# Second cross attention of a Perceiver block on one core: attention weights transposed in 32 by 32 blocks instead of by matrix multiplication

## The chip, the cores and the metric

The kernel runs on one core of a Trainium2 chip. The core has five engines that run side by side: TensorE (PE in the profile, its weight loads PEld) multiplies matrices into PSUM, VectorE (DVE), ScalarE (ACT) and GpSimd (POOL) work on elements, and SyncE (SP) issues most DMAs. Each engine executes its own instructions in program order. The metric is the device time of one execution in microseconds (us).

## What is computed

The reference is a chain of layers on `x`, 32 batches of 64 tokens with 256 features, and a context of 256 rows for each batch, all in float32. The layers are a cross attention with 16 heads of 64 (the first one), a linear attention, a gated feed forward, a second cross attention with 16 heads of 16, an sLSTM recurrence along the 64 tokens, and a mixture of 8 experts with an entmax router. The change lies in the second cross attention:

```python
Q = (query @ Wq.T + bq) ; K = (key @ Wk.T + bk) ; V = (value @ Wv.T + bv)     # 16 heads of 16
energy = einsum('bhqd,bhkd->bhqk', Q, K) / sqrt(16)
energy = where(mask == 0, -1e20, energy)
attention = softmax(energy, axis=-1)
out = einsum('bhqk,bhkd->bhqd', attention, V) ... @ Wo.T + bo
```

Since each row of `attention` sums to 1, the bias `bv` adds the same vector `bv @ Wo.T` to every token.

## The kernel before

The 2048 tokens are 16 tiles of 128 rows, two batches to a tile. First the kernel does the first cross attention for all tiles. Then come 8 groups of two tiles; for each group it does the linear attention, the feed forward, the second cross attention and the sLSTM with the router. At the end the experts run, part A over the first 12 tiles and part B over the rest.

**The planner.** The code doesn't issue instructions in the order in which it is written. `Plan` (lines 210 to 381) collects all operations with a rank (`pl.rank`), an estimated length (`PlanEngine.length`, lines 452 to 472) and their dependencies. `run` (line 299) then simulates the engines and issues at each step the operation that can start earliest, by rank among equals. Operations whose rank lies more than `ahead` over the lowest waiting one are held back; `pl.run(12.0)` on line 1863 sets that. Every instruction is issued on line 375, so all of them have the line L375 in the profile, and they are told apart by tile and shape. `either` (line 288), and `copy` by it, leave the choice between ScalarE and VectorE to the planner. `together` makes one planned piece of several matmuls, and pieces with the same `pl.lane` stay in order on TensorE. Tiles in SBUF have fixed places in one large arena, named in the lists from line 588 on: each entry has a tag, a size and one or more places, and the number of places is the number of buffers. A new tile waits until the last reader of its place is done. PSUM has eight banks, taken in any order.

**The first cross attention** already transposes its weights in blocks (`l0_scores`, line 869): VectorE transposes 32 by 32 blocks of `pr` into `bT`, and 16 moves of 32 partitions each put the blocks in their places in `pT`. Of these four go to GpSimd, four to ScalarE or VectorE, and eight are DMAs from SP. `bT` has one buffer and `pT` two.

**The second cross attention** works in units of one tile `t` and one half `c` of the heads, 32 units in all. `scores` (line 1274) multiplies queries and keys into four PSUM banks; each bank holds two heads for both batches. For each of the eight pieces of 128x256 VectorE adds the mask and takes the maximum in one operation (`tensor_tensor_reduce`, line 1298, shown as CUSTOM_DVE_ANT_0), and ScalarE takes the exponential into `pr` (`xpr`, two buffers of 2048) with the row sums. `weighted` (line 1313) then transposes the 16 blocks of 128x128 on TensorE (line 1324, PSUM tile `xpTp`), four to a bank, copies each bank to SBUF by `pl.copy` (line 1325, tile `xpT`), and multiplies by the values into `po` (line 1340, `xpo`). VectorE multiplies by the transposed reciprocal sums and adds the two heads of a pair and the values' bias in one instruction (line 1349). `projected` multiplies by the output matrix. `slstm_router` (line 1365) has its clamp, sums and product on VectorE (lines 1405 to 1415).

**Constants.** `vb` (line 1035) holds the values' bias as a column, made by a product with the identity and a sum.

Of the kernel before, what the change touches and what calls it, by code (L numbers as in the profile page):

```python
# [8 lines left out]
F32 = mybir.dt.float32  # L9
I32 = mybir.dt.int32  # L10
AF = mybir.ActivationFunctionType
ALU = mybir.AluOpType
# [197 lines left out]
class Plan:  # L210
# [12 lines left out]
    def __init__(self, tc):  # L223
        self.tc, self.ops, self.slots, self.news = tc, [], {}, []
        self.rank, self.group, self.lane, self.last = 0.0, None, None, {}
        for engine, attr in self.ENGINES.items():
            setattr(self, attr, PlanEngine(self, engine))
# [71 lines left out]
    def run(self, ahead):  # L299
# [7 lines left out]
        while todo:  # L307
# [3 lines left out]
            for op in sorted(ready, key=lambda op: op.rank):  # L311
                if short is not None and op.rank > short.rank and "PE" in op.ways and op.news:
                    continue
                if op.rank > rest[-1].rank + ahead:
                    continue
                at = 0.0
                if op.news and not self.has_room(op):
                    if "PE" in op.ways and (short is None or op.rank < short.rank) and self.has_room(op, True):
                        short = op
                    continue  # L320
                for engine, (length, _) in op.ways.items():
                    at = free[engine]
                    for other in op.before:
                        at = max(at, other.end if other.on == engine and other.end == other.done else other.done + self.HOP)
                    for t_ in op.uses:
                        at = max(at, t_.free_at)
                    key = at, op.rank
                    if best is None or key < best[0]:
                        best = key, op, engine
# [109 lines left out]
class PlanEngine:  # L439
# [34 lines left out]
    def length(engine, name, args, kw):  # L474
# [18 lines left out]
        if engine == "POOL":  # L493
            return 0.7 if n < 64 else 0.3 + 2.0e-3 * n
        return 0.18 if name == "transpose" else max(0.36, 1.67e-3 * n)
# [3 lines left out]
def kernel(ctx: ExitStack, tc: tile.TileContext, d: dict, out: bass.AP):  # L499
# [130 lines left out]
    with ExitStack() as sa:  # L630
# [31 lines left out]
        for tag, size, *at in (  # L662
# [8 lines left out]
            ("xcT", 1024, 22016, 23040), ("xkT", 1024, 24064, 25088), ("xv", 1024, 30208, 31232),  # L671
            ("xpr", 2048, 26112, 28160), ("xpT", 512, 35328, 35840, 36352, 36864), ("xne", 256, 37376, 37632, 37888),
            ("xra", 256, 38144, 38400), ("xrT", 256, 38656, 38912), ("mi", 256, 39168), ("xom", 256, 39424, 39680),
# [36 lines left out]
        def bank(shape, name):  # L710
            return banks.tile(shape, F32, tag="a", name=name)
# [143 lines left out]
        def l0_keys(b, lt, cx):  # L855
# [11 lines left out]
            return cT  # L867

        def l0_scores(b, cT, qk):

# [5 lines left out]
            pl.lane = "s"  # L876
            B_ = 32
            bT = ar.tile([P, 5, 4, 4, B_], F32, tag="bT", name=f"bT{b}")
# [32 lines left out]
            for n in range(4):  # L911
                for a in range(4):
# [4 lines left out]
                    )  # L917
                    if n == 0:
                        pl.gpsimd.tensor_copy(o, i_)
                    elif n < 2:  # L920
                        pl.copy(o, i_)
                    else:
                        pl.sync.dma_start(out=o, in_=i_)
            return pT
# [117 lines left out]
        )  # L1042
        pl.vector.tensor_reduce(vb, vd, AX.X, ALU.add)

        pl.vector.tensor_scalar(s_wp, s_wp, 0.5, None, ALU.mult)
# [228 lines left out]
        def scores(t, c, q, kT):  # L1274

            pl.lane = "sc"
            nm = f"{t}_{c}"
            pl.rank = R0 + 2 * t + c - 0.5
            sm = sp.tile([P, 2, 4], F32, tag="xsm", name=f"xsm{nm}")
            pr = ar.tile([P, 2, 4, S2], F32, tag="xpr", name=f"xpr{nm}")  # L1280
            scs = [bank([P, 2, S2], f"xsc{nm}_{j}") for j in range(4)]
            with pl.together(1.45):
                for b2 in range(2):
                    for j in range(4):
# [8 lines left out]
                        )  # L1293
            for j in range(4):
                for b2 in range(2):
                    ne = ar.tile([P, S2], F32, tag="xne", name=f"xne{nm}_{j}_{b2}")
                    nmax = sp.tile([P, 1], F32, tag="xnm", name=f"xnm{nm}_{j}_{b2}")
                    pl.vector.tensor_tensor_reduce(ne, scs[j][:, b2, :], mb, 1.0, 3.0e38, ALU.add, ALU.min, nmax)
                    pl.scalar.activation(
                        pr[:, b2, j, :], ne, AF.Exp, bias=nmax, scale=-1.0, accum_out=sm[:, b2, j : j + 1]  # L1300
                    )
# [8 lines left out]
            )  # L1310
            return ra, pr

        def weighted(t, c, ra, pr, v, oT):
            pl.lane = "w"
            nm = f"{t}_{c}"
            pl.rank = R0 + 2 * t + c
            pTs = {}
            for b2 in range(2):
                for kc in range(2):
                    pT = ar.tile([P, 4, P], F32, tag="xpT", name=f"xpT{nm}_{b2}_{kc}")  # L1320
                    pT_ps = bank([P, 4, P], f"xpTp{nm}_{b2}_{kc}")
                    with pl.together(T4):
                        for j in range(4):
                            tr(pT_ps[:, j, :], pr[:, b2, j, kc * P : (kc + 1) * P], ident)
                    pl.copy(pT, pT_ps)
                    pTs[b2, kc] = pT

# [37 lines left out]
        def slstm_router(g):  # L1365
# [49 lines left out]
            pl.vector.tensor_tensor(iz[:, :, 1:], tmp2, z, ALU.mult)  # L1415
            pl.vector.tensor_tensor_scan(flat(c_), flat(fs), flat(iz), 0.0, ALU.mult, ALU.add)
# [32 lines left out]
        for g in range(NG):  # L1449
# [3 lines left out]
            for t in range(TG * g, TG * g + TG):  # L1453
                kT, v = keys_values(t)
                oT = ar.tile([P, 2, 2, S], F32, tag="xoT", name=f"xoT{t}")
                for c in range(2):
                    ra, pr = scores(t, c, q, kT)
                    weighted(t, c, ra, pr, v, oT)
                projected(t, oT)
# [402 lines left out]
        v.tensor_copy(nbi, nbf)  # L1862
        pl.run(12.0)
        n_more = nc.values_load(  # L1864
# [69 lines left out]
```

## Time and profile before

| | us |
|---|---|
| median of three timed runs | 1628.32 (1628.05 to 1630.23) |
| time of the profiled execution | 1633.02 |
| its span, first to last instruction | 1631.3 |
| TensorE busy in it | 1579.4 |
| VectorE busy | 1088.2 |
| ScalarE busy | 693.8 |
| GpSimd busy | 422.1 |

The profiled execution has a time of its own, 4.7 us over the median of the timed runs; durations from its trace are set against this time. In the lines of the profile, `out<-in` names the written and read tiles; all arena tiles have the one name `arena`, and PSUM tiles have the names of the code (`xpTp`, `xsc`, `pu`). Behind them stand the shape, the count, the busy time in us and the mean duration of one instruction in ns. Behind the last bar stands the time that the engine sat idle just before these instructions, and what ended it. Busy time counts overlapping instructions once, so for pipelined matmuls it is less than count times mean.

### The profile page before, as it was taken

How to read it: one execution, taken by the hardware profiler on the slowest of the kernel's cores; microseconds unless marked ns; L12 is line 12 of the kernel's file. 1: busy time of each engine (PE TensorE's matmuls, PEld its weight loads, DVE VectorE, ACT ScalarE, POOL GpSimd, SP SyncE). 2: the span in 40 equal slices, each digit the busy share in tenths (PEclk: the TensorE clock that was granted, in tenths of full speed). 3: DMA queues.
4: the chain of work that ended last, by engine and by line, in shares of the span. 5: the costliest groups of instructions: out<-in, count | busy, mean ns of one | idle time of the engine just before them, and what ended most of it. 6: DMA issues, size and time to landing. Idle time of an engine off the chain costs nothing. (4 is left out here: it accounts for less than half of the span.)

```text
span 1631.3 us, 25951 instructions
## 1 busy us (share of the span) xinstructions
PE 1579.4 (97%) x9226; PEld 1106.8 (68%) x9226; DVE 1088.2 (67%) x3089; ACT 693.8 (43%) x1813; POOL 422.1 (26%) x524
## 2 busy tenths in 40 slices
PE   8999999999999999999989999999999999999996
PEld 6556656565665656666556777777777776878885
DVE  6657666676766757776755788888888788762230
ACT  4434344353533535334421454454544547432332
POOL 5123123230333223331311221221212112223342
PEclk9999999999999999999999999999999999999998
DMA  6112112121112211122121000010000220455391
GB/s 212 38 30 59 38 31 44 38 59 29 39 30 46 47 34 40 30 71 53 38 54 49 14 27 27 18 37 14 27 27 20 85 80 19 133 144 141 69 307 31
DMA packets 95601, 95.02 MB, mean 58 GB/s; under 512 B 9327, under 2 KB 85936, under 8 KB 95472
## 3 DMA queue, kind: packets, MB, share of 16 engines
q1 hardware_dynamic: 89952, 85.41, 19.2%
q0 software_dynamic: 5520, 7.94, 2.4%
q8 instruction: 74, 1.21, 0.3%
q14 instruction: 55, 0.45, 0.1%
HBM read 63.63 MB, written 7.47 MB: 44 GB/s over the span
## 5 line engine op out<-in xcount | busy, mean ns | idle before, releaser
L375 PE MATMUL pu<-arena 128*128 128x512 f32 (+1 forms) x768 | 301.0, 615 | 3.5 <-ACT arena L375 2.8
L375 PE MATMUL sc<-arena 128*128 128x320 f32 x1024 | 290.5, 436 | 0.0
L375 PEld LDWEIGHTS sc<-arena 128*128 128x128 f32 x1024 | 190.8, 190 | 95.3 <-issue 19.2
L375 ACT ACTIVATE arena<-sc,nmax 128x320 f32<-128x320 f32 x256 | 134.4, 527 | 250.3 <-DVE nmax L375 241.8
L375 PEld LDWEIGHTS pu<-arena 128*128 128x128 f32 (+1 forms) x768 | 113.9, 189 | 175.9 <-issue 159.1
L375 POOL COPY arena<-arena 32x640 f32<-32x640 f32 (+1 forms) x161 | 108.9, 676 | 404.1 <-DVE arena L375 300.4
L375 DVE TENSOR_REDUCE nmax<-sc 128x1 f32<-128x320 f32 x256 | 121.8, 484 | 105.5 <-PE sc L375 104.1
L375 POOL TENSOR_TENSOR arena<-arena 128x1024 f32<-128x1024 f32 (+3 forms) x72 | 118.5, 1646 | 166.6 <-DVE arena L375 109.7
L375 ACT ACTIVATE arena<-arena,xnm 128x256 f32<-128x256 f32 x256 | 127.1, 500 | 52.1 <-DVE xnm L375 51.9
L375 DVE COPY arena<-pu 128x512 f32<-128x512 f32 x62 | 42.7, 689 | 115.4 <-PE pu L375 115.2
L375 DVE CUSTOM_DVE_ANT_0 arena<-xsc,arena 128x256 f32<-128x256 f32 x256 | 101.2, 421 | 17.7 <-ACT arena L375 10.3
L375 DVE TENSOR_TENSOR arena<-arena,sm 128x1280 f32<-128x1280 f32 x64 | 108.1, 1690 | 2.2
L375 DVE STREAM_TRANSPOSE arena<-arena 128x512 f32<-128x512 f32 (+1 forms) x192 | 104.4, 594 | 3.6
L375 ACT COPY arena<-pu 128x512 f32<-128x512 f32 x66 | 38.4, 585 | 128.0 <-PE pu L375 128.0
L375 POOL DMA_INDIRECT out<-arena x25 | 39.6, 1585 | 102.8 <-DVE arena L375 71.2
L375 PE MATMUL pqk<-arena 64*128 64x256 f32 x512 | 63.1, 383 | 1.6 <-ACT arena L375 1.6
L375 PE MATMUL xpTp<-ident,arena 128*128 128x128 f32 x512 | 63.6, 274 | 0.9 <-ACT arena L375 0.9
L375 PE MATMUL xak<-arena 128*128 128x512 f32 x128 | 62.3, 610 | 0.0
L375 PEld LDWEIGHTS xpTp<-ident,arena 128*128 128x128 f32 x512 | 56.9, 141 | 7.2 <-DVE arena L375 2.2
L375 PE MATMUL xav<-arena 128*128 128x256 f32 x256 | 61.5, 384 | 0.0
L375 PEld LDWEIGHTS po<-arena 128*64 128x64 f32 x1024 | 55.5, 137 | 8.8 <-issue 8.3
L375 PE MATMUL mepha<-arena 128*128 128x256 f32 x256 | 60.1, 385 | 1.4 <-ACT arena L375 1.4
(395 smaller groups left out, 2800.9 us busy)
## 6 DMA issues: line engine op xcount, KB each, us to landing
arena<-in_m_w SPq DMA_DIRECT2D x26, 1024.0 KB
arena<-arena SPq DMA_DIRECT2D x256, 80.0 KB
arena<-in_ctx SPq DMA_DIRECT2D x32, 256.0 KB
arena<-in_ctxT SPq DMA_DIRECT2D x16, 512.0 KB
x<-in_x SPq DMA_DIRECT2D x16, 128.0 KB
arena<-in_l0x_wkv SPq DMA_DIRECT2D x2, 1024.0 KB
arena<-arena SPq DMA_DIRECT2D x16, 128.0 KB
out<-x SPq DMA_DIRECT2D x16, 128.0 KB
```

The lines of the kernel that those rows point to most:

```text
L375: r = getattr(real, name)(*[get(a) for a in args], **{k: get(a) for k, a in kw.items()})
```

## The change

The second cross attention gets the scheme of the first one. `scores` works batch by batch: the four exponentials of a batch go into one `xpr` tile of 1024 elements (three buffers), and VectorE transposes its 32 by 32 blocks into `xbT` (one buffer of 2048). Then 16 moves of 32x512 bring them into `xpT` (one buffer of 2048): four on GpSimd, four on ScalarE, eight by DMA from SP. `weighted` multiplies straight from there. The transposes on TensorE and their evictions are gone.

The values' bias is multiplied by the output matrix once and added to the output bias `x_bo`, with two matmuls ahead of the groups; the addition of two heads goes from VectorE to GpSimd. In seven of the eight groups four operations of the sLSTM go from VectorE to GpSimd. The context tile `xcT` has one buffer in place of two, and tiles get other places in the arena. The planner costs a GpSimd copy lower, adds 0.2 us to VectorE's key where an operation may go to ScalarE as well, and looks 10 ranks ahead instead of 12.

```diff
-                    key = at, op.rank
+                    key = at + (self.lean if engine == "DVE" and len(op.ways) > 1 else 0.0), op.rank
...
-            return 0.7 if n < 64 else 0.3 + 2.0e-3 * n
+            return 0.7 if n < 64 else 0.15 + 0.97e-3 * n if name == "tensor_copy" else 0.3 + 2.0e-3 * n
...
-            ("xcT", 1024, 22016, 23040), ("xkT", 1024, 24064, 25088), ("xv", 1024, 30208, 31232),
-            ("xpr", 2048, 26112, 28160), ("xpT", 512, 35328, 35840, 36352, 36864), ("xne", 256, 37376, 37632, 37888),
+            ("xcT", 1024, 22016), ("xkT", 1024, 23040, 24064), ("xv", 1024, 30208, 31232),
+            ("xpr", 1024, 25088, 26112, 27136), ("xbT", 2048, 28160), ("xpT", 2048, 35328), ("xne", 256, 37376, 37632, 37888),
...
+        def move(n, o, i, tight=False):
+
+            if n == 0:
+                pl.gpsimd.tensor_copy(o, i)
+            elif n == 1 and tight:
+                pl.scalar.copy(o, i)
+            elif n == 1:
+                pl.copy(o, i)
+            else:
+                pl.sync.dma_start(out=o, in_=i)
...
+        pl.vector.tensor_copy(vd, vb.unsqueeze(2).to_broadcast([P, 2, P]))
+        pl.lane = "vb"
+        pvb = bank([P, D], "pvb")
+        with pl.together(0.9):
+            for c in range(2):
+                mm(pvb, vd[:, c], x_wo[:, c, :], start=(c == 0), stop=(c == 1))
+        pl.vector.tensor_tensor(row("x_bo"), pvb, row("x_bo"), ALU.add)
...
-            for j in range(4):
-                for b2 in range(2):
+            bT = ar.tile([P, 4, 2, 2, 4, B_], F32, tag="xbT", name=f"xbT{nm}")
+            for b2 in range(2):
+                pr = ar.tile([P, 4, S2], F32, tag="xpr", name=f"xpr{nm}_{b2}")
+                for j in range(4):
...
+                pl.vector.transpose(
+                    bT[:, :, b2].rearrange("p k d j c -> p j d k c"),
+                    pr.rearrange("p j (d k c) -> p j d k c", d=2, c=B_),
+                )
+            pT = ar.tile([P, 4, 2, 2, 4, B_], F32, tag="xpT", name=f"xpT{nm}")
+            for n in range(4):
+                for a in range(4):
+                    k = (a + n) % 4
+                    move(
+                        n,
+                        pT[B_ * k : B_ * k + B_, a].rearrange("p b d j c -> p (b d j c)"),
+                        bT[B_ * a : B_ * a + B_, k].rearrange("p b d j c -> p (b d j c)"),
+                        tight=True,
                     )
...
-                    with pl.together(T4):
-                        for j in range(4):
-                            tr(pT_ps[:, j, :], pr[:, b2, j, kc * P : (kc + 1) * P], ident)
-                    pl.copy(pT, pT_ps)
...
-                                pTs[b2, kc][:, j, :],
+                                pT[:, :, b2, kc, j, :],
...
-            pl.vector.scalar_tensor_tensor(
-                oT[:, c], om[:, :, 0, :], vb[:, c : c + 1], om[:, :, 1, :], ALU.add, ALU.add
-            )
+            pl.gpsimd.tensor_tensor(oT[:, c], om[:, :, 0, :], om[:, :, 1, :], ALU.add)
...
-            pl.vector.tensor_scalar(il[:, :, :, 1:], il[:, :, :, 1:], 20.0, None, ALU.min)
+            side = pl.vector if g == NG - 1 else pl.gpsimd
+            side.tensor_scalar(il[:, :, :, 1:], il[:, :, :, 1:], 20.0, None, ALU.min)
...
-            pl.vector.tensor_tensor(tmp, m[:, :, 0:S], lf[:, :, 1:], ALU.add)
-            pl.vector.tensor_tensor(tmp, tmp, m[:, :, 1:], ALU.subtract)
+            side.tensor_tensor(tmp, m[:, :, 0:S], lf[:, :, 1:], ALU.add)
+            side.tensor_tensor(tmp, tmp, m[:, :, 1:], ALU.subtract)
...
-            pl.vector.tensor_tensor(iz[:, :, 1:], tmp2, z, ALU.mult)
+            side.tensor_tensor(iz[:, :, 1:], tmp2, z, ALU.mult)
...
-        pl.run(12.0)
+        pl.run(10.0)
```

`self.lean` is 0.2. In `l0_scores` the moves go through `move` as well, without `tight`, so they stay on the engines that they had.

More of the change, by code (lines that the diff above doesn't have):

```diff
@@ L224, in __init__ @@
         self.tc, self.ops, self.slots, self.news = tc, [], {}, []
-        self.rank, self.group, self.lane, self.last = 0.0, None, None, {}
+        self.rank, self.group, self.lane, self.last, self.lean = 0.0, None, None, {}, 0.2
         for engine, attr in self.ENGINES.items():
@@ L867, in l0_keys @@
             return cT
+        B_ = 32
+        def move(n, o, i, tight=False):
[7 more added lines that the diff above has]
+                pl.sync.dma_start(out=o, in_=i)
         def l0_scores(b, cT, qk):
             pl.lane = "s"
-            B_ = 32
             bT = ar.tile([P, 5, 4, 4, B_], F32, tag="bT", name=f"bT{b}")
@@ L917, in l0_scores @@
                     )
[L918 to L923, printed above, removed]
+                    move(n, o, i_)
             return pT
@@ L1279, in scores @@
             sm = sp.tile([P, 2, 4], F32, tag="xsm", name=f"xsm{nm}")
-            pr = ar.tile([P, 2, 4, S2], F32, tag="xpr", name=f"xpr{nm}")
             scs = [bank([P, 2, S2], f"xsc{nm}_{j}") for j in range(4)]
@@ L1298, in scores @@
                     pl.vector.tensor_tensor_reduce(ne, scs[j][:, b2, :], mb, 1.0, 3.0e38, ALU.add, ALU.min, nmax)
-                    pl.scalar.activation(
-                        pr[:, b2, j, :], ne, AF.Exp, bias=nmax, scale=-1.0, accum_out=sm[:, b2, j : j + 1]
+                    pl.scalar.activation(pr[:, j, :], ne, AF.Exp, bias=nmax, scale=-1.0, accum_out=sm[:, b2, j : j + 1])
+                pl.vector.transpose(
[11 more added lines that the diff above has]
+                        tight=True,
                     )
@@ L1310, in scores, with weighted @@
             )
-            return ra, pr
-        def weighted(t, c, ra, pr, v, oT):
+            return ra, pT
+        def weighted(t, c, ra, pT, v, oT):
             pl.lane = "w"
@@ L1316, in weighted @@
             pl.rank = R0 + 2 * t + c
[L1317 to L1321, printed above, removed]
-                    with pl.together(T4):
-                        for j in range(4):
-                            tr(pT_ps[:, j, :], pr[:, b2, j, kc * P : (kc + 1) * P], ident)
-                    pl.copy(pT, pT_ps)
-                    pTs[b2, kc] = pT
             rT = ar.tile([P, 2, P], F32, tag="xrT", name=f"xrTs{nm}")
@@ L1456 @@
                 for c in range(2):
-                    ra, pr = scores(t, c, q, kT)
-                    weighted(t, c, ra, pr, v, oT)
+                    ra, pT = scores(t, c, q, kT)
+                    weighted(t, c, ra, pT, v, oT)
                 projected(t, oT)
```

## The prediction

> **What bounds the kernel now.** I read the page's busy lines first, then the busy time by stage, then the rows of the stage that the change touches. The chain of waits holds only the last 1.3 us of this trace, so I argue from the stages.
>
> ```profile
> PE 1579.4 (97%) x9226; PEld 1106.8 (68%) x9226; DVE 1088.2 (67%) x3089; ACT 693.8 (43%) x1813; POOL 422.1 (26%) x524
> ...
> PE   8999999999999999999989999999999999999996
> ```
>
> TensorE (PE) is busy almost everywhere. The busy table by stage has, after the stretch and its length, PE, PEld, DVE, ACT and POOL, then PE's clock and the DMA share.
>
> ```profile
> 40.00:880.00 840.00, 827.57 (x3960) 519.62 (x3959) 561.67 (x1105) 342.13 (x833) 223.36 (x239) 0.99 0.20 44
> 880.00:921.00 41.00, 40.63 (x198) 29.55 (x198) 28.61 (x100) 13.08 (x32) 7.87 (x13) 1.00 0.05 15
> 921.00:1407.00 486.00, 476.79 (x3768) 357.43 (x3768) 397.74 (x1472) 255.28 (x749) 92.34 (x170) 1.00 0.11 37
> 1407.00:1632.00 225.00, 202.20 (x1148) 176.21 (x1146) 72.39 (x334) 64.32 (x161) 74.73 (x66) 0.95 0.49 138
> ```
>
> The first cross attention fills 40 to 880. The second one runs from 921 to 1407, mixed with the linear attention, feed forward and sLSTM of neighbouring groups. There PE is busy 98.1% of the time (476.79 of 486) and VectorE (DVE) 82%. So what PE no longer does is saved, as long as DVE, next in line, can keep pace. One slice of that stage shows how far this goes:
>
> ```profile
> 1380.00:1400.00 20.00, 19.35 (x202) 14.82 (x201) 17.84 (x71) 13.02 (x45) 2.67 (x8) 1.00 0.33 109
> ```
>
> At DVE 89% PE still reaches 96.8%.
>
> **What the change removes.** The rows of the transposes on PE and their evictions (busy us, then mean ns):
>
> ```profile
> L375 PE MATMUL xpTp<-ident,arena 128*128 128x128 f32 x512 | 63.6, 274 | 0.9 <-ACT arena L375 0.9
> L375 DVE COPY arena<-xpTp 128x512 f32<-128x512 f32 x60 | 40.0, 685 | 4.5 <-PE xpTp L375 4.3
> L375 ACT COPY arena<-xpTp 128x512 f32<-128x512 f32 x68 | 38.6, 587 | 39.9 <-PE xpTp L375 39.8
> ```
>
> A transpose has 274 ns, but they overlap: 63.6/512 = 0.124 us of PE each. Gone are **63.6 us of PE**, all but 0.3 us of it in the 921 to 1407 stretch, 40.0 of DVE, 38.6 of ACT, and four of the PSUM bank requests of each of the 32 units (one unit: one token tile of 128 rows and one half of the heads, `scores` and `weighted`).
>
> **What it adds.** The first cross attention already does the same thing, so nearly every price has a row:
>
> ```profile
> L375 DVE STREAM_TRANSPOSE arena<-arena 128x512 f32<-128x512 f32 x128 | 83.5, 690 | 3.6
> ...
> L375 DVE STREAM_TRANSPOSE arena<-arena 128x256 f32<-128x256 f32 x64 | 25.8, 402 | 0.0
> ...
> L375 POOL COPY arena<-arena 32x640 f32<-32x640 f32 x128 | 98.1, 766 | 304.3 <-DVE arena L375 300.4
> ...
> L375 ACT COPY arena<-arena 32x640 f32<-32x640 f32 x64 | 46.2, 722 | 18.6 <-DVE arena L375 17.2
> ```
>
> - DVE: 64 block transposes of 1024 elements. From 402 ns at 256 and 690 at 512 the slope is 1.125 ns an element, so 1.27 us each and 81 us. The shape itself is not in the trace. Bounds: two of 512 (1.38 us, 88 us), or the three that took 1.63 us end to end for 1280 elements (1.30 scaled, 83); at the low side overlap with neighbours, 75. I take 81.
> - DVE loses more: 32 value-bias additions (start-to-start 0.35 us, 11), and in seven of eight groups the clamp (0.29) and three 128x128 operations of the sLSTM (0.33 each), 9. Sum for DVE: 81 - 40 - 11 - 9 = **+21 us**, so 397.7 becomes 419.
> - The 0.2 us preference against DVE applies to operations that may go to either engine. Left on DVE there are, from the same stage, copies and biased evictions of xav, xak, xaq, xrT, laq, tr_xa and tr_sl (41 us), and norms and relus (16). Between 0 and 57 us can go to ACT; a third, 19, is my choice. DVE: about 400.
> - ACT: 128 copies of 32x512, between 585 ns (128x512 out of PSUM) and 722 (the row above); 0.60, 77 us. With -38.6 and +19 it goes from 255 to 313.
> - POOL: 128 copies. The rows 329 ns (128 elements) and 766 (640) give 0.66 us at 512: 84. The oT additions, 32 of 0.56 (128x128 row): 18. The sLSTM part, 7 times 0.65 + 3 x 0.56: 16. From 92 to 210: half idle still.
> - SP: 256 DMAs of 64 KB. In the first attention eight of 80 KB take this long to issue, and the DMA line of the window 408 to 420 (slices of 0.3 us) shows the engines done at about 414.9:
>
> ```profile
> 408.38 5.16 SPq L375 DMA_DIRECT2D arena<-arena  x8
> ...
> DMA  0000049293948667584939200000000000000000
> ```
>
>   So 0.65 us each in the queue, 165 us in all, and 6.5 us from the transpose's end to the last landing. Behind them on SP stand the context load of the next tile, the stores of x and the expert weights. The context buffer is single now: its 512 KB go out when the last xav matmul is done. At 212 GB/s (the page's first slice) that is 2.5 us, against 27 us from tile to tile (432/16): filled by other lanes, price 0, at most 16 x 2.5 = 40 if nothing fills it.
> - PE: two matmuls for the bias, 0.5 us. xpo now reads its moving side in blocks of 32 columns; pu does so already at 592 ns for 512 columns, and the plain xak has 610. Price 0.
>
> **Contention of POOL and DVE.** In the first attention the DVE multiplication over 128x1280, with two SBUF inputs, takes 1.50 us at 405.5 and 2.94 at 417.8, where POOL's 128x1024 operation runs beside it. The Trainium skill, "SBUF — State Buffer", Who interferes with whom, says why that speaks against this change: the port pair shared by VectorE and GpSimd is an exclusive lock, and whoever comes second waits out the other's instruction. Row and rule lead to the same question: how much DVE work of that kind is left. In this stage it is the two long operations after the linear attention (11 us), the relus, norms and sLSTM remainder: some 30 us. POOL's share grows from 19% to 48%, so doubled durations cost DVE at most 30 x 0.29 = 9 us. I take 0 and keep 9 for the range.
>
> A rule that speaks against the change outright: the Trainium skill, "VectorE: DVE Perf Modes", Rules for kernel authors, gives 128x128 transposes to TensorE when PSUM will do. Its table (bf16) has 390 ns on TensorE and 311 on VectorE; by these the estimate is 200 us off PE and 159 onto DVE, where the trace has 63.6 and 81, and DVE would then be the bound. The rows decide.
>
> **The wait that is new.** xbT and xpT have one buffer each. The next unit's first transpose waits until all 16 moves have read xbT; the moves wait until the unit before has been multiplied out of xpT. The waiting transpose heads DVE's queue, and behind it stand the maxima of the next scores and every eviction that frees a bank for PE. Loop at best: two transposes 2.5, landing 6.5: 9 us. A unit now has 486/32 = 15.2 us, and should have 13.6. The cover is 4.6 us a unit.
>
> **Sum.** PE's work in the stage falls to 476.8 - 63.3 = 413.5. With DVE at 92% (400 of 435), a little above the slice of 89%, I take PE at 95%: 413.5/0.95 = 435 us in place of 486, 51 us less. Behind the stage PE is again the busy engine (about 96% until 1580), so the gain is passed on. The planner's other knobs (GpSimd copy cost, look-ahead 10 in place of 12) rearrange 40 to 880 too. PE idles 12.4 us there, which bounds a gain; falling to 98.1% would cost 3.6; I take 0. The profiled execution took 1633.02 (span 1631.3); 1633.0 - 51 + 0.5 = 1582.5. The median of the timed runs is 4.7 lower, 1628.3, so the forecast is **1578 us**.
>
> **Rivals.**
> 1. *PE stays at 98.1%*: 413.5/0.981 = 421.5, gain 64.5, 1564. For it: the work of several groups is at hand to fill holes. Against: DVE comes close to full.
> 2. *DVE becomes the bound*: nothing moves to ACT, contention and queueing hold DVE at 90% of the stage: 419/0.90 = 465, gain 21, 1607. For it: DVE is at 82% already and gets more.
> 3. *Slower: the single xbT loop sets the pace.* If the steps fall in series, a unit costs eight maxima 4.0, two transposes 2.5, 6.5 to the landing, 1.1 for xpo: 14.1, plus queueing. It decides from 15.2 us a unit on; at 16.2 the stage has 518 us, 32 more: 1660. For it: before, scores came in bursts 10 to 15 us apart, and the first attention has 9.2 us between transposes' end and pu (408.4 to 417.6) with two buffers. Against: xpr has three buffers, so maxima run ahead.
> 4. *It doesn't do what it says*: the transposes surely go, but if the reordering loses in 40 to 880 what the stage gains, the time stays within 0.2%, which is about what a measurement of this kernel can tell from no change.
>
> **Chances.** Forecast (1570 to 1592) 0.50; rival 1 0.16; rival 2 0.18; rival 3 0.12; rival 4 0.04. Faster 0.50 + 0.16 + 0.18 = 0.84, same 0.04, slower 0.12. The range takes in rivals 1 and 2 with the bounds of the transposes (7), the contention (9) and the knobs (12 down): 1558 to 1612.
>
> **What would show it.** No PE row with xpTp; 64 transposes of 1.2 to 1.4 us; the second attention some 435 us long, PE near 95% and DVE near 92%. Rival 2 shows as DVE over 90% with PE under 90% and PE's idle time ended by DVE; rival 3 as the transposes waiting on DMAs, and units 15 us or more apart. I am wrong too if the stretch from 40 to 880 changes by more than 5 us.

## The result and the profile after

The changed kernel takes **1667.27 us** (median of four runs, 1664.06 to 1668.67) against 1628.18 of the kernel before on the same chip: 1.0236 times as long, with a 95% interval of 1.0217 to 1.0254. It is 39 us slower, where 50 us less were forecast. The profiled execution took 1666.6 us with a span of 1664.9.

From the page of the changed kernel, the busy times, PE's digits and the granted clock:

```profile
PE 1549.1 (93%) x8718; PEld 1065.0 (64%) x8718; DVE 1037.9 (62%) x2883; ACT 804.9 (48%) x2025; POOL 524.2 (31%) x712
...
PE   7999999999999999999988999998988887889996
...
PEclk9999999999999999999988999999999886999998
```

The transposes on PE are gone (508 matmuls fewer), but PE's busy time fell by only 30.3 us instead of 63, and its idle time (span less busy) rose from 51.9 to 115.8. Both effects show in the digits: from slice 21 on, PE is often below 9, and in six of these slices the clock is too. In the trace PE is busy for 77 us at half clock (16 before), and half of that difference, some 30 us, is the busy time that didn't go. VectorE got less busy, not more. The same stretches as before, in the same columns:

```profile
40.00:880.00 840.00, 824.66 (x3954) 516.88 (x3952) 527.73 (x1059) 368.32 (x882) 218.10 (x239) 0.99 0.20 43
...
880.00:921.00 41.00, 37.48 (x166) 25.43 (x167) 20.59 (x70) 9.42 (x17) 7.26 (x12) 0.90 0.04 13
921.00:1407.00 486.00, 429.41 (x3073) 306.20 (x3072) 371.12 (x1275) 306.13 (x824) 180.60 (x322) 0.93 0.23 63
1407.00:1632.00 225.00, 206.68 (x1252) 175.24 (x1251) 89.11 (x398) 93.20 (x241) 82.67 (x94) 0.97 0.55 154
```

On PE the first 880 us are as before. In the stretch of the second attention PE is busy 88.4% (98.1% before) at a clock of 0.93 (1.00 before): 57 us idle and, by (1 - 0.93) x 486, up to 34 us more lost to the lower clock (PE is idle in a part of that time). The new operations cost what was forecast; the groups by shape:

```profile
L375 POOL COPY arena<-arena 32x512 f32<-32x512 f32 x128 | 80.2, 626 | 91.3 <-DVE xsm L375 41.5 <-DVE arena L375 36.8 <-DMA arena<-xd,arena 7.3
L375 DVE STREAM_TRANSPOSE arena<-arena 128x1024 f32<-128x1024 f32 x64 | 79.2, 1238 | 7.2 <-DMA xd<-arena 3.9 <-ACT arena L375 1.9 <-DMA arena<-arena 1.0
L375 ACT COPY arena<-arena 32x512 f32<-32x512 f32 x128 | 78.8, 616 | 24.1 <-DVE arena L375 18.5 <-DVE t_me L375 1.8 <-DVE xsm L375 1.1
```

The row of the keys' matmuls had no idle time ahead of it before and now has the most of PE's rows in this stretch. Before and after:

```profile
L375 PE MATMUL xak<-arena 128*128 128x512 f32 x128 | 62.3, 610 | 0.0
...
L375 PE MATMUL xak<-arena 128*128 128x512 f32 x128 | 70.2, 681 | 18.1 <-DMA arena<-in_ctxT 5.6 <-DVE arena L375 5.0 <-DVE xsm L375 3.4
```

How it comes about, in the timeline of PE and of SP's queue (start and duration in us):

```profile
1016.12 1.89 PE L375 MATMUL xav<-arena 128*128 128x256 f32 x8
1021.42 3.55 PE L375 MATMUL xak<-arena 128*128 128x512 f32 x4 [3.42 <-DVE xsm L375]
```

```profile
1018.04 0.33 SPq L375 DMA_DIRECT2D arena<-in_ctxT  x1
```

The last xav of tile 3 ends at 1018.0; in that moment the load into the only context buffer is issued, it lands at 1021.3, and xak of tile 4 starts at 1021.4. The timeline names `xsm` as the releaser, but what came last is the load. Of the 15 loads behind the first, 12 are issued within 0.1 us of the end of the last xav of the tile before. And the four matmuls take 3.55 us; before, such four take 1.98. Three windows of that place tell why (PE's clock is the third column from the end):

```profile
1014.50:1018.00 3.50, 3.50 (x20) 2.85 (x19) 3.18 (x13) 2.66 (x12) 0.46 (x1) 1.00 0.00 0
1018.00:1021.40 3.40, 0.01 (x1) 0.01 (x1) 3.23 (x12) 2.17 (x5) 1.33 (x2) 1.00 0.49 157
1021.40:1025.00 3.60, 3.58 (x8) 1.06 (x8) 2.59 (x10) 0.00 (x0) 3.40 (x7) 0.53 0.34 79
```

**After 3.4 us of idling PE runs 3.4 us at half clock.** So a gap is paid for a second time in part: the four matmuls lose another 1.6 us.

For the experiments the ends of xpo of tiles 0, 12 and 15 serve as marks (us from the start of the span, from the traces). "Middle" is tile 0 to 12, "tail" tile 12 to 15, "behind" from there to the end of the span:

| kernel | xpo 0 | xpo 12 | xpo 15 | middle | tail | behind | span |
|---|---|---|---|---|---|---|---|
| before | 939.3 | 1340.2 | 1408.6 | 401 | 68 | 223 | 1631.3 |
| changed | 954.4 | 1358.5 | 1465.5 | 404 | 107 | 199 | 1664.9 |
| e1, two contexts | 949.2 | 1342.3 | 1451.4 | 393 | 109 | 209 | 1660.0 |
| e5, no moves | 947.3 | 1321.4 | 1399.3 | 374 | 78 | 216 | 1615.4 |
| e9, two xbT | 951.3 | 1317.7 | 1425.6 | 366 | 108 | 213 | 1638.6 |
| e11, tail on PE | 945.3 | 1328.9 | 1406.9 | 384 | 78 | 224 | 1630.5 |
| e12, moves alone | 948.7 | 1303.4 | 1388.9 | 355 | 86 | 220 | 1609.0 |
| e14, two xbT, tail on PE from tile 11 | 945.3 | 1311.0 | 1376.9 | 366 | 66 | 222 | 1599.0 |

In the changed kernel the middle gains nothing, although the transposes of 24 of the 32 units, 48 us, are gone from it, and the tail loses 39. Of these, 23 come back behind the last mark, because part of the experts' work has moved into the tail: their first matmul (`mepha`) starts 66 us before the last xpo ends, in the kernel before 13 us. And the first mark is 15 us late already, with PE gaps and half clock between 878 and 915 us. The 34 us of the two profiled spans are 15 ahead of the marks, 3 in the middle, and 16 in the tail and behind it.

### The profile page after: what moved, and what is told of

It is laid out like the page before. It is cut to its first block, busy times and chain, and to the rows that moved or that the text cites. A ratio compares the mean times of both kernels' runs of the same rounds, so it can differ in the third digit from the quotient of the medians.

```text
span 1664.9 us, 25608 instructions
## 1 busy us (share of the span) xinstructions
PE 1549.1 (93%) x8718; PEld 1065.0 (64%) x8718; DVE 1037.9 (62%) x2883; ACT 804.9 (48%) x2025; POOL 524.2 (31%) x712
## 5 line engine op out<-in xcount | busy, mean ns | idle before, releaser
L375 POOL COPY arena<-arena 32x640 f32<-32x640 f32 (+2 forms) x289 | 186.4, 645 | 522.2 <-DVE arena L375 345.3
L375 POOL TENSOR_TENSOR arena<-arena 128x128 f32<-128x128 f32 (+3 forms) x125 | 142.0, 1139 | 217.0 <-DVE arena L375 145.9
L375 DVE STREAM_TRANSPOSE arena<-arena 128x512 f32<-128x512 f32 (+2 forms) x256 | 183.6, 755 | 10.8 <-DMA xd<-arena 3.9
L375 ACT COPY arena<-arena 32x512 f32<-32x512 f32 (+1 forms) x211 | 138.7, 658 | 38.5 <-DVE arena L375 30.9
L375 DVE TENSOR_TENSOR arena<-arena,sm 128x1280 f32<-128x1280 f32 x64 | 96.3, 1505 | 2.2
L375 PE MATMUL xak<-arena 128*128 128x512 f32 x128 | 70.2, 681 | 18.1 <-DMA arena<-in_ctxT 5.6
L375 PE MATMUL xav<-arena 128*128 128x256 f32 x256 | 66.9, 409 | 5.4 <-DVE xnm L375 3.9
L375 ACT ACTIVATE arena<-arena 128x256 f32<-128x256 f32 (+3 forms) x59 | 23.3, 397 | 89.2 <-DVE arena L375 83.9
L375 PEld LDWEIGHTS xav<-arena 128*128 128x128 f32 x256 | 50.1, 203 | 17.4 <-DVE xnm L375 4.4
```

The lines of the kernel that those rows point to most:

```text
L375: r = getattr(real, name)(*[get(a) for a in args], **{k: get(a) for k, a in kw.items()})
```

## The experiments

Ratios are to the kernel before on the same chip, with 95% intervals. Differences in us between two kernels are differences of ratios times 1632; with these intervals they are uncertain by 3 to 6 us, with e8 by 8. The cuts shorten the tile lists to the entries that change. An edit also makes the planner write another order of everything, and e8 shows that the order alone can be worth 39 us. So a difference of 10 to 30 us between two runs shows the cause that is meant only where the trace shows its wait as well, as for the context buffer; for the others the cause is argued from several runs together.

**Which part of the change: e2, e7, e3, e4.**

e2, the kernel before:

```diff
-            ("xcT", 1024, 22016, 23040), ("xkT", 1024, 24064, 25088),
+            ("xcT", 1024, 22016), ("xkT", 1024, 24064, 25088),
```

> The kernel before with one context buffer, nothing else changed. Theory A: idle time ahead of xak appears (0 in the kernel before), and the time rises from 1628 by 25 to 40 us, most of the changed kernel's loss without any of its gain. Theories B and C: the load is filled by other work, 0 to 8 us.

Measured: 1.028 (1.0263 to 1.0297), 46 us slower. In its trace 29.5 us of idle time stand ahead of xak:

```profile
L375 PE MATMUL xak<-arena 128*128 128x512 f32 x128 | 73.3, 702 | 29.5 <-DMA arena<-in_ctxT 23.9 <-DVE xsm L375 3.7 <-DVE x L375 1.6
```

```profile
921.00:1407.00 486.00, 451.15 (x3391) 332.20 (x3390) 364.12 (x1331) 226.99 (x657) 84.50 (x156) 0.97 0.10 31
```

The rest is the clock: (1 - 0.97) x 486 is 15 us. Theory A's upper end was too low; the price of this buffer, in a kernel that keeps PE full, is gap plus half clock.

e7, the changed kernel, two contexts, with the probabilities transposed on PE again:

```diff
+                pT_ps = bank([P, 4, P], f"xpTp{nm}_{b2}_{kc}")
+                with pl.together(T4):
+                    for j in range(4):
+                        tr(pT_ps[:, j, :], pT[b2][:, j, kc * P : (kc + 1) * P], ident)
+                pl.copy(pT_, pT_ps)
```

> The changed kernel with the transposes of the probabilities back on PE as before (512 matmuls, evictions, four small buffers, two contexts); the value bias through the output projection, the additions and the sLSTM's operations on GpSimd and the planner's new settings stay. If the swap of the transposes is the whole loss: 1628 within 6 us. If the other parts of the change cost as well: 1636 or more. If they are worth something: 1620 or less.

Measured: 1.0014 (0.9999 to 1.0028). Beside transposes on PE, the other parts together are worth nothing measurable; the whole loss belongs to the swap of the transposes and what it takes in buffers.

e3, the planner's settings of before in the changed kernel:

```diff
-self.last, self.lean = 0.0, None, None, {}, 0.2
+self.last, self.lean = 0.0, None, None, {}, 0.0
...
-            return 0.7 if n < 64 else 0.15 + 0.97e-3 * n if name == "tensor_copy" else 0.3 + 2.0e-3 * n
+            return 0.7 if n < 64 else 0.3 + 2.0e-3 * n
...
-        pl.run(10.0)
+        pl.run(12.0)
```

> The changed kernel with the planner's settings of the kernel before: no preference against VectorE, GpSimd's copies costed as before, a look-ahead of 12. Theory C: 15 us or more come back (1650 or less). Theories A and B: within 8 us of 1667, because buffers and transfers are the same; idle time ahead of xak stays at 12 us or more.

Measured: 1.0322 (1.03 to 1.0343), 14 us slower than the changed kernel. Theory C falls: in the changed kernel the new settings help.

e4, the matmuls of the bias later:

```diff
-        pl.lane = "vb"
+        pl.lane, pl.rank = "vb", R0 - 1.5
...
+        pl.rank = R0 - 5.0
```

> The changed kernel with the two matmuls of the value bias given a later rank, past the load of the output projection's weights that TensorE waited for (1.93 and 1.11 us at 876 to 879). All theories: 3 us of idle time go, and up to 7 us more if the half clock at 889 came from it: 1657 to 1664. If nothing changes, those waits were covered by other work that only moved.

Measured: 1.0209 (1.0192 to 1.0226); the 4 us lie within the two intervals, so that this is not shown, though the two waits are gone from the trace.

**The context buffer in the changed kernel: e1.**

```diff
-            ("xcT", 1024, 22016), ("xkT", 1024, 23040, 24064), ("xv", 1024, 30208, 31232),
-            ("xpr", 1024, 25088, 26112, 27136), ("xbT", 2048, 28160), ("xpT", 2048, 35328),
+            ("xcT", 1024, 22016, 27136), ("xkT", 1024, 23040, 24064), ("xv", 1024, 30208, 31232),
+            ("xpr", 1024, 25088, 26112), ("xbT", 2048, 28160), ("xpT", 2048, 35328),
```

> The changed kernel with two context buffers again (the second takes the third place of the probabilities). Theory A, the single context buffer: TensorE's 18.1 us of idle time ahead of xak goes, and with it part of the 42 us that more half-clock time cost after than before; 25 to 40 us less than the changed kernel's 1667, so about 1635. Theory B, the single-buffered loop of xbT and xpT sets the pace: 5 us or less in either direction, and the idle time ahead of xak moves to other groups. Theory C, the planner's new settings: 5 us or less as well.

Measured: 1.0164 (1.0147 to 1.0181), 12 us less. Less than theory A asked for, more than B or C did. The gap is gone from its row, but the stretch hardly fills:

```profile
L375 PE MATMUL xak<-arena 128*128 128x512 f32 x128 | 63.6, 623 | 0.6 <-DVE arena L375 0.6
```

```profile
921.00:1407.00 486.00, 435.83 (x3166) 311.80 (x3164) 379.93 (x1289) 311.39 (x838) 188.30 (x333) 0.94 0.24 65
```

Theory A is true and explains a third of the loss at most. What else stops PE in this kernel? No single wait is large (the largest from 921 to 1460 us, by what is waited for, is 8.7 us of `xrT` for GpSimd). Around 1222 us three short ones come together (gaps of 1.41, 0.24 and 1.27 us in the timeline):

```profile
1218.90:1222.30 3.40, 2.03 (x37) 1.38 (x35) 3.09 (x16) 1.53 (x4) 1.43 (x2) 1.00 0.00 0
1222.30:1225.70 3.40, 1.86 (x17) 1.02 (x17) 2.10 (x10) 3.40 (x11) 1.28 (x2) 1.00 0.00 0
1225.70:1232.50 6.80, 6.02 (x17) 4.47 (x18) 2.16 (x7) 0.71 (x3) 0.00 (x0) 0.50 0.03 5
```

PE is busy 60% and 55% of two slices, and the next 6.8 us run at half clock. The Trainium skill, "TensorE: Matmul & The Clock Gate", HAM oscillation, gives as its rule that PE shouldn't idle for more than about 3.4 us. The slice length agrees; the rule is too lenient here, since no gap of these slices is over 1.5 us and the clock halves all the same. But a half idle slice doesn't always do it: the first of these two is followed by full clock, and so is this one of e14, the last run below, with PE busy 47%:

```profile
1143.42:1146.83 3.41, 1.62 (x8) 1.44 (x8) 3.28 (x15) 3.05 (x8) 1.87 (x3) 1.00 0.35 133
1146.83:1150.24 3.41, 3.17 (x29) 2.46 (x28) 2.72 (x8) 3.09 (x10) 0.00 (x0) 1.00 0.01 2
```

What decides between the two isn't shown.

**Is the written order at fault? e8.** In the changed kernel with two contexts and the later bias, eleven estimates like this one:

```diff
-            with pl.together(1.45):
+            with pl.together(1.08):
                 for b2 in range(2):
                     for j in range(4):
...
-                with pl.together(0.8):
+                with pl.together(0.51):
                     for kc in range(2):
```

> The changed kernel with two contexts, the later rank of the bias matmuls, and the planner's lengths of eleven groups of PE matmuls of this part set to what the trace shows (scores 1.08 for 1.45 us, xpo 0.51 for 0.8, linear attention 0.64 for 0.9, sLSTM gates 1.0 for 1.6, xav 1.73 for 1.8, and the like). The instructions are the same, only their order differs. Theory D: the order is written against a PE that is slower than the real one, so PE arrives early and waits; with true lengths PE's idle time between 840 and 1500 falls from 75 to below 50, fewer slices have half the clock, and the time is 1645 or less. Theory B or E: within 6 us of 1657, since no duration changes.

Measured: 1.0401 (1.0353 to 1.0449), 39 us slower than e1, with a clock of 0.89:

```profile
921.00:1407.00 486.00, 431.49 (x2959) 305.88 (x2955) 362.24 (x1217) 294.05 (x782) 173.97 (x311) 0.89 0.22 60
```

Theory D, as I had put it, falls. Only the order differs, so the order alone costs these 39 us. PE's idle time over the span hardly grows (1691.3 - 1573.5 = 118 us, in e1 112), but its busy time does by 26 us: the loss is mostly the lower clock. A reading that fits is that an order written with too long PE lengths has a reserve in it, and that without it the waits fall so that the clock halves more often. That reading isn't shown.

**Moves, block transposes and their buffers: e5, e6, e9, e10, e12.** All start from e1.

e5 leaves the moves out:

```diff
-            pT = ar.tile([P, 4, 2, 2, 4, B_], F32, tag="xpT", name=f"xpT{nm}")
-            for n in range(4):
...
+            pT = bT
...
-("xbT", 2048, 28160), ("xpT", 2048, 35328)
+("xbT", 2048, 28160, 35328)
```

> The changed kernel with two context buffers, as in the run with two contexts (1659), and without the 512 moves of 32x512 blocks: xpo multiplies the blocks where the block transposes left them, with two such buffers. It leaves out half of the transposition. Theory B, the loop of block transposes, moves and xpo sets the pace, at least in the last tiles: the 109 us from the end of xpo of tile 12 to that of tile 15 fall below 85, and the time is 1630 or less. Theory D, PE runs out of other work because its order has no reserve and its gaps halve the clock, whatever feeds xpo: 12 us or less fall away, 1647 to 1659.

Measured: 0.9887 (0.9855 to 0.9918), 45 us less than e1, and the tail falls to 78. Theory B over D: the moves, or the waiting for them, or the single xbT (e5 has two), are the larger part of the loss, 19 us in the middle and 31 in the tail, of which 7 come back behind it.

e6 leaves the block transposes out:

```diff
-                    pl.scalar.activation(pr[:, j, :], ne, AF.Exp, bias=nmax, scale=-1.0, accum_out=sm[:, b2, j : j + 1])
-                pl.vector.transpose(
-                    bT[:, :, b2].rearrange("p k d j c -> p j d k c"),
-                    pr.rearrange("p j (d k c) -> p j d k c", d=2, c=B_),
-                )
+                    pl.scalar.activation(
+                        bT[:, :, b2, :, j].rearrange("p k d c -> p d k c"),
+                        ne.rearrange("p (d k c) -> p d k c", d=2, c=B_),
+                        AF.Exp, bias=nmax, scale=-1.0, accum_out=sm[:, b2, j : j + 1],
+                    )
```

> The changed kernel with two context buffers and without the 64 block transposes on VectorE: the exponentials write straight to the places that the moves read, so the 32 by 32 blocks stay untransposed (half of the transposition is left out). VectorE loses 79 us. Theory E, VectorE's added load is what holds the stage: 25 us or more below 1659. Theory B: 5 to 10 us, the 2.5 us a unit that the transposes hold in the loop, where it binds. Theory D: 12 us or less.

Measured: 1.0341 (1.0307 to 1.0376), 29 us **slower** than e1, with the 79 us of block transposes gone from VectorE and its whole busy time 43 us lower (998.6 against 1041.5). None of the theories expected that. The exponentials now write straight to the one xbT, so it is held from the first exponential to the last move. That made me suspect the hold of this buffer, which this run alone doesn't show; as a test of VectorE's load the run is spoilt by it.

e9 gives xbT a second place:

```diff
-            ("ffh", 1536, 17920, 19456), ("sg", 512, 20992, 21504),
+            ("ffh", 1536, 17920), ("sg", 512, 19456),
...
-("xbT", 2048, 28160)
+("xbT", 2048, 28160, 19968)
```

> The changed kernel with two context buffers (1659) and with two buffers for the block-transposed probabilities; for their room the feed forward's hidden layer and its gate have one buffer each. Theory B1, the next unit's block transposes wait until the moves have read xbT, and VectorE's queue with them: 15 us or more fall away, 1644 or less, most of it in the last tiles. Theory B2, it is xpo that waits for the moves of its own unit, 6.5 us from the block transposes to the last landing, with nothing else to do: within 6 us of 1659, or slower where the feed forward now waits.

Measured: 1.0006 (0.999 to 1.0021), 26 us less than e1: as much as B1 asked for, but all of it in the middle (393 to 366) and nothing in the tail. In the trace VectorE hardly waits for the moves in the changed kernel (the transposes' row above has 1.0 us ended by their DMAs, and 3.9 by another DMA of that queue; in most units the next transposes start over 1 us after the last landing). The single buffer acts through the order: the planner can put a unit's first block transpose only behind the issue of all 16 moves of the unit before. That reading is from the code of `has_room`; the runs show the 26 us, not the way.

e10 keeps the moves, but xpo reads xbT (with two of them):

```diff
-            return ra, pT
+            return ra, bT
```

> As the run with two xbT, with all 512 moves still made, but xpo reads the block-transposed tile and not what the moves write, so that nothing waits for the moves but the buffers (half of the transposition is left out of the result's way). Theory B2, waiting for the landing: nearly all of what the run without moves gained comes, 1615 to 1628. Theory F, the work of the moves on ScalarE, GpSimd and SyncE delays other things in those queues: 1645 to 1660.

Measured: 1.0066 (1.0047 to 1.0085), 10 us slower than e9. This doesn't decide between B2 and F, because xbT is now held until xpo has read it.

e12, with two xbT as well, lets the moves copy a constant weight, so nothing waits for them:

```diff
-                        bT[B_ * a : B_ * a + B_, k].rearrange("p b d j c -> p (b d j c)"),
+                        x_wo[B_ * a : B_ * a + B_].rearrange("p a b -> p (a b)"),
...
-            return ra, pT
+            return ra, bT
```

> The run without moves (1615), with the 512 moves put back as mere work: they copy blocks of a constant weight tile into a scratch tile, so no move waits for a block transpose, no xbT waits for a move, and xpo reads xbT (half of the transposition is left out of the result's way). The feed forward's hidden layer and its gate have one buffer each, as in the run with two xbT. Theory F, the moves' work in the queues of ScalarE, GpSimd and SyncE is the price: 1630 to 1640. Theory B, the waiting for their landing and the hold of the buffers is the price: 1612 to 1622.

Measured: 0.9864 (0.9842 to 0.9886): as fast as without moves (0.9887). Theory F falls. The work of 512 moves is free here; **waiting for them costs** the 23 us that lie between e9 and e12. How these divide between xpo waiting for its landing and the hold of xbT stays open. But e10 bears on it: there xpo reads xbT as in e12, and yet e10 is 33 us slower (1.0066 against 0.9864). So the moves that stand in their queues until the transposes are done, and hold xbT until they have read it, can cost this much with no xpo waiting for a landing. The stretch in e9, in e5, then in e12:

```profile
921.00:1407.00 486.00, 443.22 (x3261) 317.75 (x3260) 388.12 (x1341) 332.28 (x894) 196.62 (x352) 0.95 0.25 68
```

```profile
921.00:1407.00 486.00, 462.08 (x3383) 331.91 (x3382) 371.48 (x1347) 267.59 (x798) 125.59 (x236) 0.95 0.13 41
```

```profile
921.00:1407.00 486.00, 457.34 (x3459) 333.00 (x3458) 393.15 (x1381) 338.79 (x917) 192.93 (x343) 0.97 0.26 71
```

**The tail: e11, e13, e14.** In the last tiles no feed forward or linear attention is left to fill PE, and the routing of the first twelve tiles, a chain of short steps over VectorE, ScalarE and PE, lies between them. What a unit's chain looks like there, in SP's queue and on PE of e1:

```profile
1328.21 0.39 SPq L375 DMA_DIRECT2D arena<-in_m_w  x1
1328.69 3.83 SPq L375 DMA_DIRECT2D arena<-arena  x6
1331.92 1.24 SPq L375 DMA_DIRECT2D arena<-arena  x2
1338.13 0.51 SPq L375 DMA_DIRECT2D arena<-arena  x1
```

```profile
1340.35 1.94 PE L375 MATMUL xpo<-arena 128*32 128x128 f32 x32 [4.88 <-DMA arena<-arena]
```

Seven of the unit's eight DMA moves are issued within 4.5 us (the sixth counts in two of the lines), behind a load of expert weights; the eighth follows at 1338.13, 5 us late. In the middle most units need 4.9 us for all eight. PE stands 4.88 us and then runs xpo slowly. What SP waited for from 1332 to 1339:

```profile
SPq L375 <- DMA arena<-in_m_w: 5.0, 1, 5.0
```

The wait ends with the landing of a load of expert weights. In the changed kernel the same wait stands in the units whose issues take longest: 3.3 us at 1291, 2.6 at 1345 and 4.2 at 1452. From the end of the block transposes to the last landing these three need 10.6 to 12.8 us, where most units need 6.4. Why a move has to wait for that load isn't shown, and a run without these loads in SP's queue wasn't made.

e11, from e1 with e4's bias:

```diff
+            blk = t < 12
...
+                if blk:
+                    pl.vector.transpose(
...
+            if not blk:
+                pTf = ar.tile([P, 2, 2, 4, P], F32, tag="xpT", name=f"xpT{nm}")
+                for b2 in range(2):
+                    for kc in range(2):
+                        pT_ps = bank([P, 4, P], f"xpTp{nm}_{b2}_{kc}")
```

> The changed kernel with two context buffers and the later rank of the bias matmuls, in which tiles 0 to 11 take the block transposes and moves, and tiles 12 to 15 are transposed on PE as before. If the loss of the tail (109 us against 68 in the kernel before, from xpo of tile 12 to that of tile 15) comes from the latency of block transposes and moves when little other PE work is left: the tail falls to 68 to 80 and the time to 1620 to 1632. If it comes from the routing of the first twelve tiles, which lies in this stretch whatever the transposes do: the tail stays above 95 and the time above 1645.

Measured: 0.9963 (0.9945 to 0.9981), 33 us less than e1, with the tail at 78 us, as expected of the latency. Of the 31 us of the tail 15 come back behind it; the middle is 9 us shorter too, and the first mark 4 us earlier.

e13 adds e9's two xbT (with one ffh and one sg) to e11.

> Two context buffers, two xbT, the later rank of the bias matmuls, tiles 0 to 11 by block transposes and tiles 12 to 15 on PE. The run with two xbT had xpo of tile 12 done at 1317.7, and the run with the tail on PE took 78 us from there to xpo of tile 15, and 224 more to its end. If the two add: 1318 + 78 + 224 is a span of 1620 at most, and 1605 to 1618 if the bias's 4 us and the shorter start of the tail come too. If the tail on PE only helped because the middle was late: 1624 to 1632.

Measured: 0.9903 (0.9882 to 0.9925), a median of 1618.38, and a span of 1621.0 in the profiled execution, the longest of the four: 1 us over what the sum allowed. 43 us less than e1, where 26 and 33 make 59; they overlap.

e14, tile 11 on PE as well:

```diff
-            blk = t < 12
+            blk = t < 11
```

> As the run before it, with tile 11 on PE as well, so that the routing of the first twelve tiles finds only PE transposes beside it. If the latency in that stretch is what is left: 2 to 8 us faster than with tile 12 as the first; if PE's work is (3.7 us a tile): 2 to 5 us slower.

Measured: **0.9787 (0.9764 to 0.9809)**, 1599.45 us, faster than both kernels, and 19 us faster than e13, where 2 to 8 were expected. Between 1260 and 1350 us PE is busy 79.63 us at a clock of 0.87 in e13 and 88.02 us at 1.00 in e14; what in tile 11 makes so much of it wasn't tried. Its page and its stretch:

```profile
PE 1534.8 (96%) x8878; PEld 1064.7 (67%) x8878; DVE 1016.9 (64%) x2869; ACT 797.0 (50%) x2019; POOL 499.6 (31%) x672
...
PEclk9999999999999999999998999999999999999997
```

```profile
921.00:1407.00 486.00, 463.19 (x3626) 343.06 (x3625) 388.99 (x1395) 329.54 (x898) 185.15 (x330) 1.00 0.25 70
```

At last the clock is 1.00. The tail in numbers, 1340 to 1440 of the changed kernel and of e14 (they hold different work):

```profile
1340.00:1440.00 100.00, 75.63 (x537) 54.15 (x531) 66.40 (x250) 56.87 (x154) 34.87 (x64) 0.78 0.33 95
```

```profile
1340.00:1440.00 100.00, 96.09 (x686) 78.46 (x685) 59.55 (x264) 48.62 (x135) 31.37 (x44) 1.00 0.43 123
```

22 of 32 units take the blocks, so 44 of the 63.6 us of PE's work are gone, and 34 of them (1633.05 to 1599.45) are in the time: a share of 0.77, where the prediction had 51 of 63.6, or 0.80. It came in the one run of blocks in which no slice of the stretch fell to half clock.

## Why the prediction was wrong, point by point

- **What bounds the kernel.** Before, PE does. After, PE stands for 57 of the 486 us and no other engine is full: the waits do. "What PE no longer does is saved, as long as DVE can keep pace" was the wrong test: VectorE kept pace at 76% of the stretch (371.12 of 486), and still nothing was saved.
- **Removed.** The 63.6 us went (no xpTp row), but PE's busy time fell by 30.3: the other 33 us are matmuls that ran longer, some 30 of them by the half clock.
- **Added work.** Right: block transposes 1238 ns (1.27 us forecast), moves 616 ns on ScalarE (0.60) and 626 on GpSimd (0.66), 6.4 us from transposes' end to the last landing in most units (for one, 1258.8 to 1265.2; 6.5 forecast). In some of the last units it was 10.6 to 12.8 us, which the prediction didn't have. The 81 us of block transposes, which the prediction sets beside 63.6 as if the trace had both, were its estimate; they measured 79.2. Costing the moves as work was right too (e12). The preference against VectorE moved more than "a third": VectorE's total fell by 50 us, 34 of them in 40 to 880, where the prediction had put nothing. The matmuls of the bias, priced at 0.5 us, also waited 1.93 and 1.11 us for their weights.
- **The single context buffer, price 0.** Failed: 12 us in the changed kernel (e1) and 46 in the kernel before (e2). "Filled by other lanes" didn't hold in the order that was written. By its code the planner lets the load start at the planned end of the last reader and counts some 4 us for it, so it knew of the wait; why it put nothing of PE's there isn't shown. My bound of 40 left the clock out, and took 2.5 us a load where issue to landing is 3.5 (median on the page).
- **The new wait, xbT: cover 4.6 us a unit.** Failed: a second buffer takes off 26 us (e9), and waiting for the moves costs 23 more (e12). The loop of 9 us was compared with the mean unit; the units come 8 to 33 us apart.
- **Sum, PE at 95%.** Failed, and this is the step that carries the error. Measured 88.4%, at a clock of 0.93, and the sum has no term for the clock at all. VectorE, from which the 95% was argued, is at 76% and not at 92. The 95% was taken from one slice that showed PE full beside a busy VectorE; what it should have asked is how much time each chain may be late before PE stands. In place of 51 us less, the runs show 12 us lost with the context buffer (e1), 26 with the single xbT (e9) and 23 with the waiting for the moves (e12), each with its half clock (differences between runs, not parts of one sum).
- **Contention and settings, price 0.** For 40 to 880 right: PE's busy time there changed by 2.9 us. Beyond it the settings are worth 14 us in the changed kernel (e3), in its favour. The 12 additions x<-arena,r_lay,x on VectorE, with two SBUF inputs, went from 482 to 544 ns, 0.7 us in all (to 755 ns in e1, 3.3 us), within the 9 us kept for it.
- **Rivals.** Rival 3 came nearest: it asked for units 16.2 us apart and 1660, and the units are 17.0 us apart (starts of the first and the last xpo, 937.0 and 1463.5, over 31; before, 15.6). That its time came so near is in part luck: its loop isn't what runs in series on the chip in the middle, and the tail, where the latency stands bare, the context buffer and the clock were not in it. Rival 2 is wrong: VectorE isn't near its limit. Rival 3's chance of 0.12 was too low because each wait was priced by itself, against a mean unit, and none with the clock.

## What to carry to other kernels

Work taken off a full engine was worth its time here only where the replacement's latency had a buffer to hide in and other work beside it. So price the buffers that a change gives up like instructions, by the gap that they open, and charge a gap on PE with more than its length: 29.5 us ahead of one group cost 46 (e2). Where a swap shortens the work but lengthens the chain, use it where other work is plentiful and keep the short chain at the end: with two contexts and two xbT, all tiles by blocks was as fast as the kernel before (e9), and tiles 0 to 10 by blocks with the rest on PE 2.1% faster (e14).

## What the runs showed of the hardware

- PE's granted clock falls to half for 3.4 us (changed kernel, 1021.6 to 1025.0) or a multiple of it (e1, 6.8 us from 1225.7). Half clock followed a slice with PE busy 55%, with no gap over 1.5 us (e1, 1222.3), but not one with 60% (e1, 1218.9) or 47% (e14, 1143.4); after an idle slice of 3.4 us four matmuls took 3.55 us instead of 1.98.
- 512 moves of 32x512 elements, 128 each on ScalarE and GpSimd and 256 by DMA, cost no time when nothing waited for them (0.9864 against 0.9887 without them).
- Eight DMA issues in SP's queue, 4.9 us in most units, took up to 9.9 us in the last ones (e1), where loads of 1 MB of expert weights stand in the same queue. In the longest, SP stood 5.0 us until such a load had landed.
